# Last row-mode fetch moved ahead, mode sums joined before the root, a new order of tail loads and single-bank PSUM tiles in a two-layer block on a 512 x 512 x 64 image

## The chip, the cores and the metric

The kernel runs on one core of one Trainium2 chip. The metric is the device time of one execution in microseconds (us); before the change it is 1838.84 us, the median of three runs (1837.78 to 1840.75). The engines are named as in the profile: PE is the matrix engine (PEld its weight loads), DVE the vector engine, ACT the scalar engine, POOL the engine that here multiplies, adds and issues gathers, SP the engine that issues most of the DMAs.

## What is computed

The input x is 1 x 512 x 512 x 64 in fp32. Two layers follow one another, each added to its own input after a group norm with 32 groups of two channels over the whole image:

```python
x = x + conv0(gn(x), sequence_mask, ...)   # layer norm over channels, left and right projections with gates,
                                           # einsum('bkjd,bkid->bijd', left, right), layer norm, projection, output gate
x = x + conv1(gn(x), w_real, w_imag)

def conv1(x):                              # spectral convolution
    x_ft = fft2(x over rows, columns)[:12, :12]
    out_ft = einsum('bcmn,comn->bomn', x_ft, w_real + 1j * w_imag)
    return real(ifft2(out_ft put into zeros of 512 x 512))
```

Only 12 x 12 modes of the second layer's transform are kept, so it is done as matrix products with small tables of cosines and sines. Its group norm is linear in x except for its mean and scale: the modes are taken of the raw sums, and the scale (and at mode 0 the mean) is put in at the end. Both are known only once all of layer 0's output has been made. So the kernel ends with a stage in which nothing of the output can be written until the statistics and the modes of the whole image are there.

## The kernel before

The masked rows are fewer than 257 here, so the branch `compact` runs. Its main loop (about L1119 to L1231) walks over steps s, with k and n from `divmod(s, 8)`: n is the step within a unit of layer 0, and v counts the 32 output units, `last` being 31. A unit is one tile of 32 columns of the image by half of its rows. Inside this loop `tc.manual_schedule()` holds: each engine gets its instructions in the order in which the code writes them. In each step the code writes, among others, these pieces, each for its own unit and with its own delay:

- `times` (L979): the output gate's product w_ps on PE, for this step;
- `transform` (L1069): the row transform f_ps of the unit before, on PE at n = 0 and n = 4;
- the sigmoid on ACT (L1146) at even n; `gated` (L1038) and `added` (L1042) on POOL, and for the last quarter of the last unit `finished` (L1050, L1053) on DVE;
- `save` (L1077) copies f_ps on ACT and writes it to modes_d in DRAM (L1091), for the column tile before the last one on ACT's DMA queue; for the last column tile it goes straight on with 16 matmuls (L1083) into the PSUM tile `ends[0]`;
- `fetch(h)` (L904) reads a block of modes_d back with columns of the image on partitions, `columns(h)` (L896) transforms along the columns into t_ps; for h = 3 the block has 96 rows, comes on ACT's queue and is left open in `ends[0]`, so that L1083 adds the last 32 columns to it;
- `prepare` (L912): 24 small ACT operations, 6 in each of the steps n = 2 to 5 of the last unit, that spread the basis of the last column tile for L1083;
- `statistics` (L1097): DVE's batch statistics of the unit before; the joins L1102 to L1115 combine them;
- the gate's products z_t on DVE: `w_ps` by the factor (L1195) and the bias (L1201);
- `store` (L1058): layer 0's result to DRAM (x_h) by SP; `fetch_rows` (L629): a gather of a finished tile of x_h back into a buffer, issued by POOL, 15 of them ahead of their use (`AHEAD`). A buffer is one of four in the ring of `places`, in five tiles lx_t, in a spare piece, or earlier ones.
- w_real and w_imag, 2304 KB each, are read by SP (L1231) at v = last - 1, n = 3.

Behind the loop stands the tail (L1233 to L1372). It clears `picks` (L1237), lists the remaining load buffers and issues their gathers, loads three small tables, and calls `group_norm_affine` (L241) with the hook `turn_sums`. That sums the chunk means (`part`, L251), multiplies by an averaging matrix (mean_ps, L253), makes the mean (L255) and the variance (var_ps, L265), runs the hook (L1255 on DVE adds `ends[0]` to the sums, L1256 on PE turns them), then takes the inverse root (`rsqrt`) and picks each partition's own value. The rest joins the real and imaginary parts into v_modes (L1263, L1264), scales them into `picks` (L1267, L1273), multiplies by the mode weights (mixed_ps, L1282), sums (L1288, L1292), transforms back along the columns in `back_columns` (q_ps L1309, its copies L1320 on DVE and L1322 on ACT, transposes it_ps L1327, copies L1330 and L1332) and last, for 64 output tiles, along the rows (l_ps, L1348), adds to the loaded x (L1355) and stores (L1356); each tile issues the gather 15 tiles ahead.

Two lines of the call order matter for the change. In the loop:

```python
if (v, n) == (last, 4):
    fetch(3)
if (v, n) == (last, 7):
    ends.append(columns(3, ps_t))
```

These stand at the end of the code of a step, so behind that step's `times`, sigmoid, `prepare`, `statistics` and z_t products.

Of the kernel before, what the change touches and what calls it, by code (L numbers as in the profile page):

```python
# [46 lines left out]
def conv_preact_kernel(ctx: ExitStack, tc: tile.TileContext, t: dict):  # L47
# [192 lines left out]

    def group_norm_affine(keep, sets, each, name, between=lambda: None):  # L241


        groups, n = sets[0].shape[1:]
        avg = avg_p if groups == G else avg_c
        ab = keep.tile([P, 3], F32, name="ab_" + name)
        with tc.tile_pool(name="gn_" + name, bufs=1) as gp, tc.tile_pool(
            name="gnp_" + name, bufs=1, space=PSUM
        ) as gps:
            part = gp.tile([P, groups], F32, name="part")  # L250
            nc.vector.tensor_reduce(part, sets[0], AX.X, ALU.add)  # L251
            mean_ps = gps.tile([P, groups], F32, name="mean_ps")
            nc.tensor.matmul(mean_ps, avg, part, start=True, stop=True)  # L253
            mean = gp.tile([P, groups], F32, name="mean")
            nc.vector.tensor_scalar(mean, mean_ps, 1.0 / (n * each), None, ALU.mult)  # L255
            d = gp.tile([P, groups, n], F32, name="gn_d")
            nc.vector.scalar_tensor_tensor(
                d, sets[0], 1.0 / each, mean.unsqueeze(2).to_broadcast([P, groups, n]), ALU.mult, ALU.subtract
            )
            nc.vector.tensor_mul(d, d, d)  # L260
            nc.vector.scalar_tensor_tensor(d, sets[1], 1.0 / each, d, ALU.mult, ALU.add)
            v = gp.tile([P, groups], F32, name="v")
            nc.vector.tensor_reduce(v, d, AX.X, ALU.add)
            var_ps = gps.tile([P, groups], F32, name="var_ps")
            nc.tensor.matmul(var_ps, avg, v, start=True, stop=True)  # L265
            between()
            rs = rsqrt(gp, var_ps, 1.0 / n, EPS, [P, groups])
            if groups == G:
                mine = gp.tile([P, 2, G], F32, name="mine")
                nc.vector.tensor_mul(mine[:, 0, :], rs, pick)  # L270
                nc.vector.tensor_mul(mine[:, 1, :], mean, pick)
                am = gp.tile([P, 2], F32, name="am")
                nc.vector.tensor_reduce(am, mine, AX.X, ALU.add)
                rs, mean = am[:, 0:1], am[:, 1:2]
            nc.vector.scalar_tensor_tensor(ab[:, 1:2], mean, -1.0, rs, ALU.mult, ALU.mult)
            nc.vector.tensor_copy(ab[:, 0:1], rs)
            nc.vector.tensor_scalar(ab[:, 2:3], mean, -1.0, None, ALU.mult)
        return ab
# [334 lines left out]
    def compact(fc):  # L613
# [193 lines left out]
        with tc.tile_pool(name="tri", bufs=1) as trp:  # L807
# [57 lines left out]
            with tc.manual_schedule(), tc.tile_pool(name="late", bufs=1) as lp:  # L865
# [65 lines left out]
                with tc.tile_pool(name="np_x", bufs=LEAD + 2) as tp, tc.tile_pool(  # L931
# [189 lines left out]
                    for s in range(-LEAD, total_g + 2 * SIZE):  # L1121
# [101 lines left out]
                        if n == 6 and v % 8 == 3 and 8 < v < len(units):  # L1223
                            columns(v // 8 - 1, ps_t)
                        if (v, n) == (last, 4):
                            fetch(3)
                        if (v, n) == (last, 7):
                            ends.append(columns(3, ps_t))
# [4 lines left out]
                with tc.tile_pool(name="lq", bufs=1) as qp, tc.tile_pool(name="lx", bufs=1) as xp:  # L1233

                    picks = qp.tile([P, MODES, 3, 32], F32, name="picks")
                    fetch_rows(len(fetched))
                    nc.gpsimd.memset(picks, 0.0)  # L1237
                    buffers += [xp.tile([P, JC, C], F32, name=f"lx_t{i}") for i in range(5)]
                    buffers += [place(i)[:, r * JC : (r + 1) * JC] for i in (0, 1) for r in range(2)]
                    spare = places[:, 7 * 64 * C - 8 * 2 * MODES * M2 : 7 * 64 * C]  # L1240
# [9 lines left out]
                    with tc.tile_pool(name="sps", bufs=1, space=PSUM) as sps:  # L1250
# [9 lines left out]

                        ab2 = group_norm_affine(lp, sets, 8, "x1c", turn_sums)
                        v = qp.tile([P, 2, MODES, MODES], F32, name="v_modes")
                        nc.vector.tensor_add(v[:, 0], sums[:, :, :MODES], turned[:, :, MODES:])  # L1263
                        nc.vector.tensor_sub(v[:, 1], turned[:, :, :MODES], sums[:, :, MODES:])  # L1264
                        for k in range(2):
                            for q in range(3):
                                nc.vector.tensor_scalar(  # L1267
                                    picks[:, :, q, 12 * k + 4 * q : 12 * k + 4 * q + 4], v[:, k, :, 4 * q : 4 * q + 4],
                                    ab2[:, 0:1], None, ALU.mult,
                                )  # L1270
                            h = slice(k * C, (k + 1) * C)
                            one = picks[h, 0, 0, 12 * k : 12 * k + 1]
                            nc.vector.scalar_tensor_tensor(one, ab2[h, 1:2], float(N * N), one, ALU.mult, ALU.add)  # L1273

# [3 lines left out]
                        for m3 in range(3):  # L1278
                            for q in range(3):
                                for g in range(4):  # L1280
                                    m = MODES // 4 * g + m3
                                    nc.tensor.matmul(  # L1282
                                        mixed_ps[32 * g : 32 * g + 32, m3].rearrange("p (o g) r -> p o g r", g=4),
                                        picks[:, m, q, :], by_mode[:, :, :, m * MODES + 4 * q : m * MODES + 4 * q + 4],
                                        start=(q == 0), stop=(q == 2), tile_position=(0, 32 * g),
                                    )
                        own = picks.rearrange("p m q k -> p (m q k)")[:, : 3 * C * 4].rearrange("p (c r) -> p c r", r=4)
                        nc.vector.tensor_mul(  # L1288
# [11 lines left out]
                    def back_columns(jb, pq, pt, first):  # L1300

                        it = parts[:, jb // 2, : 256 * 16].rearrange("p (j o) -> p j o", o=16)
                        for g2 in range(2):
                            ps = pq.tile([P, 2, 4, 2, C], F32, name="q_ps")[:, :, :3]
                            for part in range(2):
                                for i in range(2):
                                    g = 2 * g2 + i
                                    h = slice(32 * g, 32 * g + M2)
                                    nc.tensor.matmul(  # L1309
                                        ps[:, i, :, part, :], col_inv[h, part, jb, :], mixed[h],  # L1310
                                        start=True, stop=True, tile_position=(32 * g, 0),
                                    )
                            for i in range(2):
                                g = 2 * g2 + i
                                src = ps[:, i].rearrange("p m k o -> p (m k) o")
                                for k, q in enumerate(qs):
                                    dst = q[:, :, 6 * g : 6 * g + 6].rearrange("p o r -> p r o")
                                    o = k * C // 2
                                    if first and k == 0:
                                        nc.vector.tensor_copy(dst, src[:, :, o : o + C // 2])  # L1320
                                    else:
                                        nc.scalar.copy(dst, src[:, :, o : o + C // 2])  # L1322
                        for o4 in range(4):
# [7 lines left out]
                            else:  # L1331
                                nc.scalar.copy(dst, ps)  # L1332
                    with tc.tile_pool(name="lpq0", bufs=2, space=PSUM) as pq, tc.tile_pool(
                        name="lpt0", bufs=4, space=PSUM
                    ) as pt:
                        back_columns(0, pq, pt, True)
                    with tc.tile_pool(name="lpq", bufs=1, space=PSUM) as pq, tc.tile_pool(
                        name="lpt", bufs=2, space=PSUM
# [103 lines left out]
```

## Time and profile before

| what | us |
|---|---|
| median of three runs | 1838.84 |
| profiled execution | 1839.54 |
| its span, first to last instruction | 1837.7 |
| PE busy | 1637.7 (89%) |
| DVE busy | 1423.6 (77%) |
| ACT busy | 961.9 (52%) |
| POOL busy | 945.3 (51%) |
| column transform L896 of the last fetch, start | 1501.48 |
| mean_ps L253, start | 1517.42 |
| mixed_ps L1282, start | 1526.97 |
| first copy of q_ps L1320, start | 1537.57 |
| first output store L1356, start | 1549.93 |

The profile is of one execution. The span is the time from its first instruction to its last. The rows of slices cut the span in 40 equal parts of 45.9 us; a digit is the share in tenths. The DMA row is the mean busy share of the 16 DMA engines. A timeline line has start, length, engine (with a q where it is the engine's DMA issue), line, operation, output and input with shapes, the count and in square brackets the idle time just before it with what ended it. A line of the chain has start, length and the piece. The clock row, PEclk, is the clock granted to PE as a share of full speed. Over the whole span DMA moves 467.94 MB in 188453 packets.

### The profile page before, as it was taken

The page shows a single profiled execution, that of the slowest core. Times are in us where ns is not written, and L with a number is a line of the kernel's source. Part 1 is how long each engine was busy: PE and PEld are TensorE (multiplying, and loading weights), DVE is VectorE, ACT ScalarE, POOL GpSimd, SP SyncE. Part 2 cuts the span into 40 slices and gives each one's busy share as a digit, 9 for nine tenths or more (in the row PEclk, how much of TensorE's full clock was granted, in tenths as well). Part 3 has the DMA queues.
Part 4 walks back from the last instruction along what each step waited for, and adds up shares of the span by engine and source line. Part 5 has one row for each costly group of instructions (what it writes and reads, how often), then busy time and mean ns, then how long its engine had stood idle before and what let it go on. Part 6 is the DMA issues. An engine that isn't in the chain of part 4 may idle for free.

```text
span 1837.7 us, 33577 instructions
## 1 busy us (share of the span) xinstructions
PE 1637.7 (89%) x11414; PEld 1287.7 (70%) x11414; DVE 1423.6 (77%) x2973; ACT 961.9 (52%) x1708; POOL 945.3 (51%) x711
## 2 busy tenths in 40 slices
PE   6779799999799999999999999999999866998772
PEld 5667666665678878897788888888888744665441
DVE  5989777777455547788999999999999975675552
ACT  3555555555222259976777777777777631111000
POOL 3666211111000006788999999999999862211110
PEclk9989899999899999999999999999999966555555
DMA  6999255556656513667777876776777698999999
GB/s 255 381 375 371 106 127 138 138 138 154 208 174 182 177 41 141 224 234 257 254 244 249 279 269 233 241 274 234 253 258 258 210 273 338 411 426 426 427 427 379
DMA packets 188453, 467.94 MB, mean 255 GB/s; under 512 B 34672, under 2 KB 134000, under 8 KB 147184
## 3 DMA queue, kind: packets, MB, share of 16 engines
q1 hardware_dynamic: 157376, 262.21, 42.5%
q0 software_dynamic: 27712, 201.40, 29.1%
q10 hardware_dynamic: 3184, 2.08, 0.4%
q8 instruction: 93, 1.52, 0.3%
q14 instruction: 88, 0.72, 0.1%
HBM read 278.05 MB, written 187.56 MB: 253 GB/s over the span
## 4 chain that ended last, share of the span: by engine, by line
PE 29%; DVE 16%; DMA 9%; POOL 4%; issue 3%; ACT 1%; DVEq 0%; POOLq 0%; ACTq 0%
PE c_ps L979 6%; PE w_ps L979 6%; PE t_ps L969 5%; PE l_ps L1348 4%; DVE stats2c L1097 4%; DMA places<-x_h,dst_i 4%; PE y_ps L990 4%; DVE z_t L1195 3%; DVE scratch L1012 3%; DVE z_t L1201 3%; PE f_ps L1069 2%; POOL z_t L1038 2%; DMA out_x<-places 2%; POOL places L1042 2%; DMA lx_t<-x_h,dst_i 2%
## 5 line engine op out<-in xcount | busy, mean ns | idle before, releaser
L979 PE MATMUL w_ps<-gate_x,xt_c 128*128 128x128 f32 x2048 | 280.1, 280 | 32.1 <-DVE z_t L1195 26.7
L1042 POOL TENSOR_TENSOR places<-places,z_t 128x1024 f32<-128x1024 f32 x127 | 301.2, 2371 | 8.0
L979 PEld LDWEIGHTS w_ps<-gate_x,xt_c 128*128 128x128 f32 x2048 | 251.5, 194 | 47.8 <-DVE z_t L1195 43.4
L979 PE MATMUL c_ps<-center_x,xt_c 128*128 128x128 f32 x2048 | 276.2, 278 | 1.2 <-ACT xt_c L1008 0.6
L979 PEld LDWEIGHTS c_ps<-center_x,xt_c 128*128 128x128 f32 x2048 | 252.1, 194 | 3.9 <-ACT xt_c L974 2.3
L1348 PE MATMUL l_ps<-places,rinv 24*128 24x512 f32 x512 | 207.8, 1124 | 29.3 <-DVE places L1355 18.6
L1097 DVE BATCH_NORM_STATS2 stats2c<-places 128x6 f32<-128x128 f32 x1024 | 220.5, 278 | 12.5 <-POOL places L1042 12.5
L1012 DVE TENSOR_REDUCE scratch<-sq_c 128x16 f32<-128x1024 f32 x160 | 194.6, 1216 | 27.9 <-ACT sq_c L1007 18.7
L1146 ACT ACTIVATE z_t<-z_t 128x1024 f32<-128x1024 f32 x128 | 135.5, 1059 | 133.7 <-DVE z_t L1201 116.0
L1199 POOL TENSOR_TENSOR z_t<-z_t,bias_row_out 128x1024 f32<-128x1024 f32 x32 | 75.7, 2365 | 246.6 <-DVE z_t L1195 242.5
L969 PE MATMUL t_ps<-c_ident,places 128*128 128x128 f32 x1280 | 199.0, 278 | 1.3 <-DVE places L854 1.3
L1348 PEld LDWEIGHTS l_ps<-places,rinv 24*128 24x128 f32 x512 | 120.3, 303 | 111.9 <-DVE places L1355 59.6
L969 PEld LDWEIGHTS t_ps<-c_ident,places 128*128 128x128 f32 x1280 | 144.5, 142 | 60.6 <-issue 50.3
L974 ACT ACTIVATE xt_c<-t_ps,ab_xc 128x512 f32<-128x512 f32 x256 | 176.0, 687 | 10.7 <-PE t_ps L969 9.8
L1195 DVE TENSOR_TENSOR z_t<-w_ps,rs_n 128x512 f32<-128x512 f32 x256 | 171.9, 672 | 3.7 <-PE w_ps L979 3.5
L1004 ACT ACTIVATE sq_c<-c_ps 128x512 f32<-128x512 f32 x256 | 150.5, 588 | 30.9 <-PE c_ps L979 29.4
L679 DVE BATCH_NORM_STATS2 stats1c<-x_ps 128x6 f32<-128x512 f32 x256 | 155.6, 681 | 12.5 <-PE x_ps L678 12.2
L1201 DVE TENSOR_TENSOR z_t<-z_t,scratch 128x1024 f32<-128x1024 f32 x128 | 156.3, 1221 | 10.0 <-ACT rs_n L1018 3.8
L1038 POOL TENSOR_TENSOR z_t<-z_t,places 128x1024 f32<-128x1024 f32 x64 | 151.6, 2369 | 16.2 <-ACT z_t L1146 13.3
L1355 DVE TENSOR_TENSOR places<-places,l_ps 128x512 f32<-128x512 f32 x176 | 110.2, 683 | 56.1 <-DMA places<-x_h,dst_i 45.5
L1038 POOL TENSOR_TENSOR z_t<-z_t,bias_row_out 128x1024 f32<-128x1024 f32 x63 | 149.4, 2371 | 4.6 <-ACT z_t L1146 4.0
L733 POOL COPY rbc<-rq_out 128x512 f32<-128x512 f32 x64 | 38.3, 613 | 210.0 <-DVE rq_out L209 132.0
(212 smaller groups left out, 2748.8 us busy)
## 6 DMA issues: line engine op xcount, KB each, us to landing
x_h<-places SPq DMA_DIRECT2D x64, 1024.0 KB
out_x<-places SPq DMA_DIRECT2D x44, 1024.0 KB
places<-u_d SPq DMA_DIRECT2D x512, 64.0 KB
out_x<-lx_t SPq DMA_DIRECT2D x20, 1024.0 KB
left_d<-o_c SPq DMA_DIRECT2D x64, 256.0 KB
right_d<-o_c SPq DMA_DIRECT2D x64, 256.0 KB
left_raw<-left_d SPq DMA_DIRECT2D x64, 256.0 KB
right_raw<-right_d SPq DMA_DIRECT2D x64, 256.0 KB
```

The source lines that it names most:

```text
L679: nc.vector.bn_stats(stats[:, 0, 16 * (jc % quarter) + 4 * r + c, :], ps.rearrange("p i k -> p (i k)"))
L969: nc.tensor.transpose(tps[:, i, :], flat[:, o : o + P], ident)
L974: nc.scalar.activation(xts[s], tps, AF.Identity, bias=ab1[:, 2:3])
L979: nc.tensor.matmul(ps[:, 2 * i : 2 * i + 2, :], xts[s][:, i, :], w, start=True, stop=True)
L1004: nc.scalar.activation(sq, cps, AF.Square)
L1012: nc.vector.tensor_reduce(totals[k % 2][:, 8 * (n - 1) : 8 * (n + 1)], sqs.pop(s // 2), AX.X, ALU.add)
L1038: nc.gpsimd.tensor_mul(zs[k, c], zs[k, c], u)
L1042: nc.gpsimd.tensor_add(xr, xr, zs.pop((k, c)))
L1097: nc.vector.bn_stats(st[k // 4][:, g, k % 4, :], x_of(k)[:, :, 2 * g : 2 * g + 2])
L1195: nc.vector.tensor_mul(z[:, 8 * odd : 8 * odd + 8, :], wps, rs)
L1201: nc.vector.tensor_add(z, z, bias_ps["ogate"].unsqueeze(1).to_broadcast([P, 16, C]))
L1348: nc.tensor.matmul(ps.rearrange("p j o -> p (j o)"), rinv[h, b, :], it[h], start=True, stop=True, tile_position=(32 * g, 0),)
```

## The change

1. In the last unit, `fetch(3)` stands in the code of n = 0 instead of n = 4, and `columns(3)` in that of n = 6 instead of n = 7.
2. `group_norm_affine` has two hooks. `with_mean` runs after the mean's product, and gets `turn_sums`. `with_variance` runs after the variance's product and before the root; the partition's own mean is picked before it, and it gets the new `join_modes`: the two v_modes operations and the two that put the mean in at mode 0 (into v, ahead of the scale). After the root, only the scale is picked and multiplied in. `picks` has a row of 108 places for a mode (three blocks of 36, with a window of 32 at 32 q), so that two operations of 128 x 144 take the place of six of 128 x 48 and two one-element ones.
3. The list of load buffers begins with the two halves of place 0, then the five lx_t, then place 1 and the spare piece; before, the five lx_t came first.
4. Each q_ps group has its own PSUM tile of one bank (four buffers for the first `back_columns`, two later); before, two groups shared a tile of two banks. In the first `back_columns`, DVE copies both halves of one group and ACT both of the other; before, DVE copied one half of each and ACT the other.

```diff
-    def group_norm_affine(keep, sets, each, name, between=lambda: None):
+    def group_norm_affine(keep, sets, each, name, with_mean=lambda: None, with_variance=lambda ab: None):
...
             nc.tensor.matmul(mean_ps, avg, part, start=True, stop=True)
+            with_mean()
...
             nc.tensor.matmul(var_ps, avg, v, start=True, stop=True)
-            between()
+            if groups == G:
+                mine = gp.tile([P, 2, G], F32, name="mine")
+                nc.vector.scalar_tensor_tensor(mine[:, 1, :], mean, -1.0, pick, ALU.mult, ALU.mult)
+                nc.vector.tensor_reduce(ab[:, 2:3], mine[:, 1, :], AX.X, ALU.add)
+            else:
+                nc.vector.tensor_scalar(ab[:, 2:3], mean, -1.0, None, ALU.mult)
+            with_variance(ab)
             rs = rsqrt(gp, var_ps, 1.0 / n, EPS, [P, groups])
             if groups == G:
-                mine = gp.tile([P, 2, G], F32, name="mine")
                 nc.vector.tensor_mul(mine[:, 0, :], rs, pick)
-                nc.vector.tensor_mul(mine[:, 1, :], mean, pick)
-                am = gp.tile([P, 2], F32, name="am")
-                nc.vector.tensor_reduce(am, mine, AX.X, ALU.add)
-                rs, mean = am[:, 0:1], am[:, 1:2]
-            nc.vector.scalar_tensor_tensor(ab[:, 1:2], mean, -1.0, rs, ALU.mult, ALU.mult)
-            nc.vector.tensor_copy(ab[:, 0:1], rs)
-            nc.vector.tensor_scalar(ab[:, 2:3], mean, -1.0, None, ALU.mult)
+                nc.vector.tensor_reduce(ab[:, 0:1], mine[:, 0, :], AX.X, ALU.add)
+            else:
+                nc.vector.tensor_copy(ab[:, 0:1], rs)
+            nc.vector.tensor_mul(ab[:, 1:2], ab[:, 2:3], ab[:, 0:1])
...
-                        if (v, n) == (last, 4):
+                        if (v, n) == (last, 0):
                             fetch(3)
-                        if (v, n) == (last, 7):
+                        if (v, n) == (last, 6):
                             ends.append(columns(3, ps_t))
...
-                    picks = qp.tile([P, MODES, 3, 32], F32, name="picks")
+                    picks = qp.tile([P, MODES, 3 * 36], F32, name="picks")
...
-                    buffers += [xp.tile([P, JC, C], F32, name=f"lx_t{i}") for i in range(5)]
-                    buffers += [place(i)[:, r * JC : (r + 1) * JC] for i in (0, 1) for r in range(2)]
+                    for i in (0, 1):
+                        buffers += [place(i)[:, r * JC : (r + 1) * JC] for r in range(2)]
+                        if i == 0:
+                            buffers += [xp.tile([P, JC, C], F32, name=f"lx_t{j}") for j in range(5)]
...
-                        ab2 = group_norm_affine(lp, sets, 8, "x1c", turn_sums)
                         v = qp.tile([P, 2, MODES, MODES], F32, name="v_modes")
-                        nc.vector.tensor_add(v[:, 0], sums[:, :, :MODES], turned[:, :, MODES:])
-                        nc.vector.tensor_sub(v[:, 1], turned[:, :, :MODES], sums[:, :, MODES:])
+
+                        def join_modes(ab):
+                            nc.vector.tensor_add(v[:, 0], sums[:, :, :MODES], turned[:, :, MODES:])
+                            nc.vector.tensor_sub(v[:, 1], turned[:, :, :MODES], sums[:, :, MODES:])
+                            for k in range(2):
+                                h = slice(k * C, (k + 1) * C)
+                                one = v[h, k, 0, 0:1]
+                                nc.vector.scalar_tensor_tensor(one, ab[h, 2:3], float(N * N), one, ALU.mult, ALU.add)
+
+                        ab2 = group_norm_affine(lp, sets, 8, "x1c", turn_sums, join_modes)
                         for k in range(2):
-                            for q in range(3):
-                                nc.vector.tensor_scalar(
-                                    picks[:, :, q, 12 * k + 4 * q : 12 * k + 4 * q + 4], v[:, k, :, 4 * q : 4 * q + 4],
-                                    ab2[:, 0:1], None, ALU.mult,
-                                )
-                            h = slice(k * C, (k + 1) * C)
-                            one = picks[h, 0, 0, 12 * k : 12 * k + 1]
-                            nc.vector.scalar_tensor_tensor(one, ab2[h, 1:2], float(N * N), one, ALU.mult, ALU.add)
+                            nc.vector.tensor_scalar(
+                                picks.rearrange("p m (q f) -> p m q f", q=3)[:, :, :, 12 * k : 12 * k + 4],
+                                v[:, k].rearrange("p m (q j) -> p m q j", q=3), ab2[:, 0:1], None, ALU.mult,
+                            )
...
-                                        picks[:, m, q, :], by_mode[:, :, :, m * MODES + 4 * q : m * MODES + 4 * q + 4],
+                                        picks[:, m, 32 * q : 32 * q + 32], by_mode[:, :, :, m * MODES + 4 * q : m * MODES + 4 * q + 4],
...
-                            ps = pq.tile([P, 2, 4, 2, C], F32, name="q_ps")[:, :, :3]
+                            pair = [pq.tile([P, 4, 2, C], F32, name="q_ps")[:, :3] for _ in range(2)]
...
-                                        ps[:, i, :, part, :], col_inv[h, part, jb, :], mixed[h],
+                                        pair[i][:, :, part, :], col_inv[h, part, jb, :], mixed[h],
...
-                                src = ps[:, i].rearrange("p m k o -> p (m k) o")
+                                src = pair[i].rearrange("p m k o -> p (m k) o")
...
-                                    if first and k == 0:
+                                    if first and i == 0:
                                         nc.vector.tensor_copy(dst, src[:, :, o : o + C // 2])
...
-                    with tc.tile_pool(name="lpq0", bufs=2, space=PSUM) as pq, tc.tile_pool(
+                    with tc.tile_pool(name="lpq0", bufs=4, space=PSUM) as pq, tc.tile_pool(
...
-                    with tc.tile_pool(name="lpq", bufs=1, space=PSUM) as pq, tc.tile_pool(
+                    with tc.tile_pool(name="lpq", bufs=2, space=PSUM) as pq, tc.tile_pool(
```

## The prediction

> **What bounds the kernel now.** I read first the page's slices, then a table of stretches of the tail, then the chain of waits in order of time, then the timeline of the last two units. In the slices, the row of DMA shares:
>
> ```profile
> DMA  6999255556656513667777876776777698999999
> ```
>
> The DMA is full in the last eight slices but for one dip. The stretches (length, busy time of PE, PEld, DVE, ACT, POOL, then clock, DMA share, GB/s) show where it is not:
>
> ```profile
> 1490.00:1495.00 5.00, 0.00 (x0) 0.00 (x0) 4.57 (x13) 2.36 (x4) 4.92 (x3) 0.50 0.80 159
> 1540.00:1545.00 5.00, 3.65 (x16) 3.27 (x16) 2.47 (x3) 2.26 (x3) 0.00 (x0) 0.50 0.83 346
> 1545.00:1550.00 5.00, 3.92 (x14) 2.05 (x15) 2.48 (x4) 0.26 (x1) 0.00 (x0) 0.50 0.04 16
> 1550.00:1837.70 287.70, 220.73 (x598) 134.13 (x594) 157.39 (x252) 20.02 (x36) 45.89 (x49) 0.51 0.99 413
> ```
>
> From the first output store (1549.93) to the end the DMA is full: 64 stores and 49 loads of 1 MB each. Just before, it is empty: all early loads have landed and no store has begun. So the end is the first store plus a constant 288 us, and what counts is when the first store comes. The chain leads back from it:
>
> ```profile
> 1485.32 16.11 DMA places<-modes_d
> 1501.48 5.31 PE t_ps L896 x24
> 1506.80 3.67 PE f_ps L1069 x16
> 1510.49 0.59 ACT places L1077
> 1511.12 6.37 PE t_ps L1083 x32
> 1517.49 0.60 PE mean_ps L253 x2
> ```
>
> The mean waits on PE behind L1083 and everything ahead of it, and that waits for the last fetch of row modes. The statistics path is ready earlier: `part`, L251, is done at 1512.82, while mean_ps runs at 1517.42. It is next in line, 4.6 us behind. The timeline says how the fetch came to take 16 us, and what else stands near:
>
> ```profile
> 1468.40 1.80 ACTq L1091 DMA_DIRECT2D modes_d<-places  x4
> 1478.80 1.06 ACT L1146 ACTIVATE z_t<-z_t 128x1024 f32<-128x1024 f32 x1 [2.94 <-DVE z_t L1201]
> 1481.52 0.47 SPq L1231 DMA_DIRECT2D places<-in_w_imag  x1
> 1485.32 0.33 ACTq L904 DMA_DIRECT2D places<-modes_d  x1
> 1487.91 1.68 PE L979 MATMUL w_ps<-gate_x,xt_c 128*128 128x128 f32 x8 [0.21 <-DVE z_t L1195]
> 1491.18 0.68 DVE L1195 TENSOR_TENSOR z_t<-w_ps,rs_n 128x512 f32<-128x512 f32 x1
> 1501.48 5.31 PE L896 MATMUL t_ps<-col_basis,places 96*128 96x24 f32 x24 [11.89 <-DMA places<-modes_d]
> 1526.71 0.16 DVE L1273 SCALAR_TENSOR_TENSOR picks<-ab_x1c,picks 64x1 f32<-64x1 f32 x1 [1.77 <-DVE picks L1267]
> 1537.57 0.48 DVE L1320 COPY q_sb<-q_ps 128x192 f32<-128x192 f32 x1 [1.68 <-PE q_ps L1309]
> 1538.09 0.48 ACT L1322 COPY q_sb<-q_ps 128x192 f32<-128x192 f32 x1 [26.47 <-DVE q_sb L1320]
> ```
>
> The modes_d writes that the fetch reads are issued at 1468.40 to 1470.2, but w_imag and the last unit's stores, which wait for the first and the last of them, leave SP at 1481.52 and 1482.73: the writes lie behind w_real (2304 KB, 64 packets, issued 1461.95), and their queue moves its packets between 1476.4 and 1481.4. So fetch(3), wherever it stands, cannot issue before 1481.5 to 1482.7. Before, ACT issued it at 1485.32.
>
> **What the Trainium skill says.** "DMA: Bandwidth & Descriptors", section "Queues, rings and completion order": each DMA engine goes round its queues packet by packet and drains a whole packet before it turns. The trace agrees: w_imag's four packets per engine end at about 1483.1, 1485.5, 1488.3 and 1491.3 to 1494, and of the fetch's 112 packets 5 move in 1490 to 1494, 58 in 1494 to 1498, 49 until 1501.4. "TensorE: Matmul & The Clock Gate", part 2: matmuls stay in program order, only weight loads are pulled ahead; its part 1: after an idle window the array runs at half clock. The trace shows 0.50 after 1490. "PSUM — Partial Sum Buffer", section "PSUM bank collisions raise a hardware error": reads of one bank by two engines are kept apart by a dependency. The trace shows L1320 and L1322 strictly in turn.
>
> **Part 1: fetch and columns moved.** The fetch issues at 1482.0 to 1482.7 instead of 1485.32, 3 us earlier. ACT reaches it at 1475.9, right behind the last unit's first sigmoid, and waits; the next sigmoid (1478.80) slips to about 1482.5, and the 12 spreads behind it (4.26 us), then POOL's products: POOL is busy throughout, so it slips 0.6 to 1.2 us, off the path. The fetch arrives during w_imag's first packets instead of its third. As the later fetch did, it lets about two pass first, sends one packet per engine near 1491, a second before 1494; the remaining 80 or so go at the 14.5 per us that 58 in 4 us gave, against the same stores and gather: 5.5 to 6.3 us, so landing L = 1499.5 to 1500.3. I take L = 1500.3. Bounds: 1494.5 if w_imag alternates fairly from its first packet, 1501.4 if the start gains nothing.
>
> The columns now stand on PE between w_ps of the last unit's n = 6 and n = 7; before, after both. So w_ps(n=7), done by 1489.6 in the cover of the fetch, now waits for the fetch too, and behind it DVE's z_t (1491.18), the sigmoid, L1050, L1053 and 40 statistics (end 1504.49: 13.3 us from z_t on). Step by step: columns L to L+5.35 (5.31 measured); w_ps at half clock 1.97 (1.68 measured at mixed clock), z_t at L+7.3; 13.3 to the end of the statistics, L+20.6; joins 1.6 (1504.49 to 1506.10); square .6 on ACT, which before stood queued behind the save; between .5, part .4 and its gaps, L+24.1; mean L+24.8. L1083 ends only at about L+20.6 (w_ps, f_ps 3.7, save .6, L1083 6.4 and gaps), so statistics decide. Before, mean was at 1518.12. With L = 1500.3 it is 1525.1: 7.0 later. The clear loss of part 1.
>
> **Part 2: sums and mean joined ahead of the root.** Mean to `v` stays 2.02 us (1518.12 to 1520.14): L+26.8. The picked mean, its sum, v_modes (.21 each step) and two one-element operations run while var_ps is made, and push the root .6: it starts at L+27.9, lasts 1.98 (1520.64 to 1522.62), L+29.9. After it stand one product, a sum, a product and two picks of 128x144: 1.27 from the like rows, mixed_ps at L+31.15. Before: root end to mixed_ps 4.35 us, of which 1.77 is the stall in front of L1273 beside a POOL gather. So 2.3 to 2.5 net, 0.7 if such a stall comes back. Price bounds: -2.5 to -0.5.
>
> **Part 3: PSUM tiles.** Copies of q_ps go from 3.4 us in turn (1537.57 to 1540.95) to two engines side by side, 1.5 us: the first it_ps starts 1.75 earlier, bounds 0 (PE or clock takes it) to 1.9.
>
> **Part 4: load order.** Place 0's loads need only the statistics of unit 30 and its store; lx_t need `part` as before. Two megabyte loads move from after lx_t to about L+14. Hidden: the nine loads finish at about 1549, still before the first store; 3 us margin. Uncovered it would be 4.9 us per load and store pair. The larger memset (+0.13 us by 1296 to 1152 elements) lies in POOL's idle 13 us. Cost 0.
>
> **Sum.** mixed_ps before 1526.97, after L+31.15 = 1531.45: +4.5. Part 3: -1.75. First store 1549.93 + 2.7 = 1552.6; span 1837.7 + 2.7 = 1840.4, execution 1839.54 + 2.7 = 1842.2. That execution is .7 above the median of 1838.84; on the median 1841.5. In one line: change = L - 1497.6.
>
> **Rivals.** 0.2% is 3.7 us, about what measurement can tell from no change.
> (a) My forecast: L 1498.5 to 1501.2, +1 to +3.7: 1841.5. Chance .40. For it: the packet pattern; against: two queues' phase is one sample.
> (b) Other side, slower: the fetch gains nothing, or the stall before the picks comes back, or the PSUM gain is lost. L = 1501.4 gives +3.8, 1842.7; with a stall of 1.77 on top 1844.4. It decides from L = 1501.3. For it: x_h stores and two gathers meet the fetch at the same time as before (DMA 348 GB/s in 1495 to 1500). Chance .35.
> (c) Faster: the fetch gets its turns ahead of w_imag and lands by 1488, when w_ps(n=7) is due at 1487.91. Then the change is 1488 - 1497.6 = -9.6: 1829. It decides below L = 1493.9. Against: ACT cannot issue before 1481.5, and w_imag is out by then. Chance .14.
> (d) L 1494 to 1498.5: 1837, no difference. Chance .08.
> (e) The change doesn't reach the end, because the stores are DMA bound whatever the first one does: 1838.8. Against it the hole of 16 GB/s. Chance .03.
>
> **How the numbers follow.** Faster .14 (c), same .51 (a, d, e), slower .35 (b). Range 1834 to 1846.5: it leaves out most of (c), some .12, and .06 above, where stalls add up. The likeliest case's own range is 1839.8 to 1842.5.
>
> **What the changed profile would show.** Right: ACT issues the fetch at 1482 to 1483 right before a late sigmoid; PE's columns wait for places<-modes_d with w_ps behind them; DVE idles before the last z_t to about 1507; L1083 no longer ends last before mean_ps, the statistics do; statistics end near 1521; no gap before the picks; L1320 and L1322 overlap; the hole of the DMA before the first store, now near 1552.6. Wrong: a fetch that lands before 1494, or w_ps(n=7) ahead of the columns (then the change is at least 7 us better), or a hole filled by late loads.

## The result and the profile after

The changed kernel takes 1842.53 us, the median of 15 runs (1841.11 to 1845.06), and the kernel before 1834.81 us over 15 runs (1832.5 to 1841.76): ratio 1.0035, 95% interval 1.0024 to 1.0045, which is 6.4 us slower (0.0035 x 1834.81; 4.4 to 8.3). The time forecast was 1841.5, and the range 1834 to 1846.5; the forecast change was only +2.7 us, under the 3.7 us that the forecast took for what can be told from no change. So the time came out nearly as stated while the change came out more than twice as large. Both can be, since the median of before that the forecast started from (1838.84, three runs) is 4.0 us above the median of fifteen. That the time lies only 1.0 us from the forecast is therefore luck: a start 4.0 us too high and a change 3.7 us too small nearly cancel.

In the profile after (execution 1844.57 us, span 1842.8) the whole program has moved against the first profile of before by 3.7 us before the change's first instruction: w_real is issued at 1465.67 instead of 1461.95. Over the profiles of this study that issue lies anywhere between 1458.75 and 1466.46, whatever the kernel. So times within the tail are given below from the issue of w_real.

The timeline of the changed kernel, with the lines that answer to those shown of before (line numbers are those of its own file, up to 9 larger):

```profile
1465.67 0.52 SPq L1234 DMA_DIRECT2D places<-in_w_real  x1
1485.17 0.47 SPq L1234 DMA_DIRECT2D places<-in_w_imag  x1
1485.73 0.38 ACTq L907 DMA_DIRECT2D places<-modes_d  x1
1486.21 1.06 ACT L1149 ACTIVATE z_t<-z_t 128x1024 f32<-128x1024 f32 x1 [6.64 <-POOL places L1045]
1504.69 5.31 PE L899 MATMUL t_ps<-col_basis,places 96*128 96x24 f32 x24 [13.29 <-DMA places<-modes_d]
1509.83 2.06 PE L982 MATMUL w_ps<-gate_x,xt_c 128*128 128x128 f32 x8
1511.92 0.69 DVE L1198 TENSOR_TENSOR z_t<-w_ps,rs_n 128x512 f32<-128x512 f32 x1 [16.95 <-PE w_ps L982]
1517.45 7.81 DVE L1100 BATCH_NORM_STATS2 stats2c<-places 128x6 f32<-128x128 f32 x40
1528.86 0.61 PE L253 MATMUL mean_ps<-part,c_avg_p 128*128 128x32 f32 x2 [5.39 <-DVE part L251]
1546.19 1.45 DVE L1329 COPY q_sb<-q_ps 128x192 f32<-128x192 f32 x4 [1.02 <-PE q_ps L1318]
1546.23 1.45 ACT L1331 COPY q_sb<-q_ps 128x192 f32<-128x192 f32 x4 [18.70 <-PE q_ps L1318]
1555.51 8.88 SPq L1365 DMA_DIRECT2D out_x<-places  x4
```

The order that the forecast gave is there. ACT issues the fetch right behind w_imag, and its sigmoid has waited 6.64 us. PE stands 13.29 us for the fetch, with w_ps behind the columns; DVE stands 16.95 us for that w_ps. The statistics end at 1525.26, and mean_ps now waits for DVE's `part`, no more for the 32 products of L1083 (here L1086), which end at 1523.48. The two engines copy q_ps at the same time.

The chain of waits of the changed kernel leads from the statistics to `part` and the mean, where before it had columns, transform, save and L1083 ahead of the mean. Its last steps:

```profile
1528.30 0.43 DVE part L251
1528.73 0.14 issue
1528.86 0.62 PE mean_ps L253 x2
```

One sign went the other way. The forecast expected the DMA hole ahead of the first store to stay, with the loads of x done 3 us before it, and named a hole filled by late loads as a sign of being wrong. In before's first profile DMA was 0.04 busy there; here it is busy almost to the store:

```profile
1550.00:1555.00 5.00, 3.14 (x18) 1.87 (x17) 3.01 (x5) 1.46 (x2) 0.00 (x0) 0.84 0.93 385
```

The loads that wait for `part` are issued 12 us later after w_real than in before, and the last of them end about 0.5 us ahead of the store. It cost nothing that can be seen: from the first store to the end it is 287.3 us; in before, 287.8. The hole is no fixed part of the kernel before either (see e1).

### The profile page after: what moved, and what is told of

It reads as the page before. It is cut to its first block, busy times and chain, and to the rows that moved or that the text cites. A ratio compares the mean times of both kernels' runs of the same rounds, so it can differ in the third digit from the quotient of the medians.

```text
span 1842.8 us, 33577 instructions
## 1 busy us (share of the span) xinstructions
PE 1639.4 (89%) x11414; PEld 1289.6 (70%) x11414; DVE 1423.9 (77%) x2968; ACT 961.3 (52%) x1708; POOL 945.2 (51%) x711
```

## The experiments

Parts are numbered as in the prediction: part 3 is the PSUM tiles (item 4 in "The change"), part 4 the load order (item 3). Each kernel was timed in turn with before on the same chip, but not all on one chip, so that a difference between two of them is a difference of two ratios to before; changes in us are the ratio's difference from 1 times the median of before there (1832.8 to 1836.4).

### e1: before, once more (no edit)

> The kernel before, unchanged, for a second profile of it and for what two equal programs differ by. Theory T (the tail's order of work explains the change): ratio 1.000 within 0.001; the tail from the issue of w_real to the first output store is 88.0 us long (1461.95 to 1549.93 in the first profile), within 1 us. Rival R (the first profile of before was an unlucky one, and most executions of before have a shorter tail): the same tail is 3 us or more shorter, the fetch of 96 row modes landing nearer to 10 us after its issue than 16.

Measured: ratio 0.9996 (0.9986 to 1.0007). The second profile of the very same program has a tail 6.2 us shorter: 1460.81 to 1542.61, 81.8 us, against 88.0. Of its chain of waits:

```profile
1484.21 16.04 DMA places<-modes_d
1500.29 5.32 PE t_ps L896 x24
1505.61 3.20 PE f_ps L1069 x16
1508.83 0.59 ACT places L1077
1509.47 4.17 PE t_ps L1083 x32
```

T held for the ratio and fell for the tail. The fetch takes as long as in the first (16.04 and 16.11), so rival R was right that the tail can be shorter, and wrong on the cause. The difference up to the mean, 3.0 us, shows first in the transform (3.20 instead of 3.67 us), and for the most part at L1083: 4.17 instead of 6.37 us. The stretches that span L1083, of before's first profile and of this second one, give the clock (the column after POOL's busy time):

```profile
1511.12:1517.42 6.30, 6.30 (x32) 3.95 (x33) 1.13 (x3) 0.50 (x2) 3.38 (x4) 0.64 0.76 228
```

```profile
1509.47:1513.57 4.10, 4.10 (x33) 3.25 (x33) 1.14 (x3) 0.49 (x2) 1.79 (x2) 1.00 1.10 344
```

The granted clock was 0.64 there and 1.00 here, for the same 32 products. The 0.64 is a mean of 0.50 and a late 1.00 in before's first profile; in the second profile the clock was still 0.50 in the transform, and rose ahead of L1083:

```profile
1511.12:1515.60 4.48, 4.48 (x20) 2.90 (x22) 1.13 (x3) 0.50 (x2) 1.88 (x2) 0.50 0.70 209
1515.70:1517.42 1.72, 1.72 (x16) 0.94 (x13) 0.00 (x0) 0.00 (x0) 1.42 (x2) 1.00 0.93 276
```

```profile
1505.70:1508.05 2.35, 2.35 (x12) 0.43 (x12) 0.00 (x0) 0.00 (x0) 0.00 (x0) 0.50 1.00 422
```

So it rose 14.2 us after the columns' start in the one and 7.8 in the other. In each of the fourteen profiles all changes of the granted clock lie whole multiples of 3.41 us apart, and where this grid falls differs from one execution to the next. Seven profiles keep before's order on PE and have the columns at 5.3 us. In four of them (e1, e3, e6, e7) a grid point fell 7.7 to 8.3 us after the columns' start, the clock rose there, and L1083 took 4.17 us. In three (before's first, e4, e8) the grid points fell at 6.3 to 7.4 and again at 9.7 to 10.8, the clock rose only at 13.1 to 14.2, and L1083 took 5.8 to 6.4 us. So the first profile of before was no rare accident, but one of two kinds that come about equally often here. That the place of the grid decides is read from these seven; no run here moves it.

The points of the tail, in us after w_real's issue:

| | before, first profile | before, second | changed |
|---|---|---|---|
| columns of the fetch start | 39.5 | 39.5 | 39.0 |
| mean | 56.2 | 53.2 | 63.8 |
| mixing (mixed_ps) | 65.0 | 60.3 | 70.0 |
| q_ps | 74.1 | 68.5 | 79.6 |
| it_ps | 78.6 | 72.4 | 81.8 |
| l_ps | 83.4 | 77.2 | 86.2 |
| first store | 88.0 | 81.8 | 89.8 |

Between mean and mixing another 1.7 us go: the stall of 1.77 us in front of L1273 isn't there in the second profile. Of six profiles with the old order of these operations (before twice, e2, e7, e8, e10) two have it (before's first and e8), and their mean to mixing is 8.9 and 8.8 us; the others have 7.1 to 7.5.

In the second profile the DMA is nearly without a hole, with no later loads: the loads run nearly up to a first store that simply comes earlier (1542.61, 81.8 us after w_real):

```profile
1537.00:1542.60 5.60, 3.85 (x13) 2.01 (x14) 2.57 (x5) 0.94 (x1) 0.00 (x0) 0.50 0.84 348
```

The changed kernel's first store is 8.0 us after that of the second profile, and 1.9 us after that of the first. The measured 6.4 lies between the two, nearer the second.

### e2: part 1 alone

```diff
-                        if (v, n) == (last, 4):
+                        if (v, n) == (last, 0):
                             fetch(3)
-                        if (v, n) == (last, 7):
+                        if (v, n) == (last, 6):
                             ends.append(columns(3, ps_t))
```

> Before with part 1 alone: fetch(3) at n = 0 and columns(3) at n = 6 of the last unit; joins, load order and PSUM tiles as before. T: the mean comes 7 us later and nothing gives it back: +7.0 us, ratio 1.0038 (+5.5 to +8). If the rest of the change only looks like a gain in the tail and is worth nothing at the end (rival N), e2 equals the changed kernel: +6.4, ratio 1.0035, and e3 equals before.

Measured: 1.0047 (1.0032 to 1.0062), +8.6 us. The mean comes 63.8 us after w_real, exactly where it comes in the changed kernel; against before's second profile that is 10.6 us later, against the first 7.6. T's +7.0 was the cost against the first profile; the measured 8.6 lies between the two. Rival N said +6.4 here and 0 for the next kernel; this one's interval (+5.9 to +11.4) doesn't exclude it, the next one's does.

### e3: the change without part 1

> The changed kernel with part 1 undone: fetch(3) at n = 4 and columns(3) at n = 7 as before; the joined sums, the load order and the PSUM tiles stay. T: mean_ps waits for L1083 as in before, then 2.3 us less to the mixing and 1.8 us less in the copies: -3.5 to -4.1 us, ratio 0.998. Rival N: 0, ratio 1.000. Rival M (something outside of the tail makes the changed program start its main loop later, as its profile shows a shift of 3.7 us before the change's first instruction): 0 to +2 us with the shift of 3.7 us in its profile again.

Its edit is the diff above, backwards, on the changed kernel. Measured: 0.9976 (0.9965 to 0.9986), -4.4 us. T is right, N and M are out: the other three parts make the kernel faster, and part 1 more than takes it away (10.8 us between the two ratios, 6.4 + 4.4). In its profile the fetch lands 38.8 us after w_real, the mean comes at 52.8, and the shift of the main loop is not there (w_real at 1461.05). The chain from the mean on is shorter by what the steps said and by one thing more, in the timeline:

```profile
1530.96 1.94 PE L1336 MATMUL it_ps<-c_ident,q_sb 128*128 128x128 f32 x16 [1.24 <-ACT q_sb L1331]
1534.00 1.14 PE L1357 MATMUL l_ps<-places,rinv 24*128 24x512 f32 x8 [1.10 <-ACT places L1341]
```

In before's profiles these two took 3.65 and 2.09 us. PE is granted its full clock here (1.00 in 1530 to 1535).

### e4: only the columns put back behind w_ps

```diff
-                        if (v, n) == (last, 6):
+                        if (v, n) == (last, 7):
                             ends.append(columns(3, ps_t))
```

on the changed kernel; the fetch stays early.

> The changed kernel with columns(3) alone put back to n = 7, behind the last product w_ps; the fetch stays at n = 0. T: no wait on the statistics' path any more; the fetch lands 0.5 us earlier than in before, so -4 to -4.7 us against before, 10 us better than the changed kernel: ratio 0.9977. If the early fetch itself costs (the sigmoid behind it on ACT is late, and POOL with it, rival A): between -1 and +3.

Measured: 0.9965 (0.9953 to 0.9977), -6.4 us against before (-8.6 to -4.2; T had said -4 to -4.7). Against the changed kernel that is 12.8 us from the place of one call. Of these the two profiles show 9.6: the first store comes 80.3 us after w_real instead of 89.8, and the mean 54.8 instead of 63.8, although L1083, back on the path, had a clock of 0.70 in this profile and took 5.8 us. Its timeline shows w_ps of both last steps ahead of the wait, and the columns alone behind it:

```profile
1478.89 0.38 ACTq L907 DMA_DIRECT2D places<-modes_d  x1
1483.37 3.68 PE L982 MATMUL w_ps<-gate_x,xt_c 128*128 128x128 f32 x16 [1.47 <-DVE z_t L1198]
1497.67 5.32 PE L899 MATMUL t_ps<-col_basis,places 96*128 96x24 f32 x24 [10.63 <-DMA places<-modes_d]
```

The early fetch lands 38.9 us after w_real, later fetches 38.8 (e3) and 39.5 (before, twice): from issue to landing it takes 18.8 us instead of 15.4 to 16.1. Issuing it 3 us earlier gains next to nothing, and rival A (-1 to +3) is out: the intervals of this kernel and of e3 overlap and show no cost of the early fetch.

### e9: w_imag behind the fetch, in the changed kernel

```diff
-                        if v == last - 1 and n == 3:
-                            for part, name in enumerate(("w_real", "w_imag")):
-                                nc.sync.dma_start(wide[part * C : (part + 1) * C], ...)
+                        if v == last - 1 and n == 3:
+                            mode_weights(0, "w_real")
...
                         if n == 6 and v - 1 == last:
-                            for r in range(2):
-                                store(last, r)
+                            store(last, 0)
+                            mode_weights(1, "w_imag")
+                            store(last, 1)
```

> The changed kernel with only the load of w_imag moved, from right behind w_real to between the last unit's two stores, so that it can't be issued before the fetch of the row modes. T (w_imag's packets hold the fetch back, and the fetch holds w_ps): the fetch lands 5 to 7 us after its issue instead of 19, the columns no longer make w_ps late by more than 4 us, and the changed order costs next to nothing: -4 to -8 us against before, 11 to 16 us better than the changed kernel. Rival S (the stores and gathers hold the fetch, w_imag doesn't matter): as the changed kernel, +6 to +8.

Measured: 0.9977 (0.9969 to 0.9985), -4.2 us against before. From its timeline:

```profile
1482.36 0.33 ACTq L907 DMA_DIRECT2D places<-modes_d  x1
1489.16 5.06 PE L899 MATMUL t_ps<-col_basis,places 96*128 96x24 f32 x24 [0.92 <-DMA places<-modes_d]
1494.05 2.05 PE L982 MATMUL w_ps<-gate_x,xt_c 128*128 128x128 f32 x8
1494.96 0.48 SPq L1059 DMA_DIRECT2D places<-in_w_imag  x1
```

The fetch lands 6.8 us after its issue instead of 19.0, with the first of the last unit's stores and the gathers about as before: w_imag held it. The changed order of PE is still in place, but PE waits 0.92 us for the fetch, and the change becomes a gain, at the low end of T's range. Rival S is out.

### e10 and e14: PE kept busy until the fetch lands

```diff
+                    for _ in range(24 if h == 3 else 0):
+                        nc.tensor.matmul(
+                            ps.rearrange("p m n -> p (m n)"), turn, sums.rearrange("p m n -> p (m n)"), start=True, stop=True
+                        )
                     for m in range(MODES):
                         nc.tensor.matmul(ps[:, m, :], by[:q, m, :], col_basis[:q, h, :], ...)
```

once on before and once on the changed kernel.

> Before with 24 extra products of turn and sums (128 x 288 each, overwritten by what follows) on PE ahead of columns(3), in the time in which PE waits for the fetch; nothing else. T2 (the clock of PE at the landing of the fetch sets how long columns, transform and L1083 take, and is why before's first profile was 6 us longer in the tail than its second): mean_ps no later than 13 us after the columns' start, -1 to -3 us against before, and no spread of several us between executions of the tail. Rival C (the clock is no matter, or the products don't hold it): 0, or later if they outlast the wait.

Measured on before: 0.9981 (0.9969 to 0.9992), -3.5 us. The columns take 2.86 instead of 5.3 us, and mean_ps starts 12.5 us after them (first and second profile of before: 15.9 and 13.3). But the clock, 1.00 through the columns, fell to 0.50 within the transform behind them; L1083 ran at 0.66 in this profile and took 6.2 us, and the first store (81.6 us after w_real) is no earlier than in before's second profile. So the gain and the shorter columns of T2 are shown; that the spread of the tail would go is not: L1083 can still meet the low clock, and the times lie between 1825.9 and 1835.9 us.

> The changed kernel with the 24 extra products ahead of columns(3), as in e10, so that PE stays at full clock until the fetch lands. T: columns 2.9 instead of 5.3 us and w_ps 1.2 instead of 2.1, both on the path of the changed kernel: 3.3 us better than it, so +3 to +5 against before, ratio 1.0020. Rival: the clock of PE is no part of the loss, +6.4 as the changed kernel.

Measured on the changed kernel: 1.0023 (1.0014 to 1.0032), +4.2 us (2.6 to 5.9), so some 2.2 of its 6.4 us (4.4 to 8.3) gone, though the intervals overlap. In the profiles the first store comes 2.1 us earlier (87.8 instead of 89.8 us after w_real). Its columns and w_ps, from the timeline:

```profile
1503.34 2.76 PE L903 MATMUL t_ps<-col_basis,places 96*128 96x24 f32 x24
1505.93 1.68 PE L986 MATMUL w_ps<-gate_x,xt_c 128*128 128x128 f32 x8
```

The statistics end 56.5 us after w_real, in the changed kernel 59.6: 3.1 of the 3.3 us that were expected at that point.

### e7, e6 and e8: each of the other parts alone, on before

> Before with part 3 alone, each q_ps group in a PSUM bank of its own. T as predicted: the copies end 1.75 us sooner: -1.8 us, ratio 0.9990. T2, after the profile of the kernel without part 1 (where the transposes it_ps also took 1.94 instead of 3.65 us): the shorter gap also leaves PE at full clock in what follows, -3 to -4.4 us, ratio 0.998. Rival N: 0.

Part 3 (the q_ps hunks of the diff): 0.9980 (0.9971 to 0.9988), -3.7 us. The copies are over sooner by what was forecast (q_ps to it_ps 2.19 us instead of 3.96 in before's second profile). The time is in T2's range, but its own profile shows the faster clock only in part, with it_ps at 3.15 us and l_ps at 2.09: 1.76 and 0.5 us together are 2.3, just inside the interval (-5.3 to -2.2). In the six profiles without part 3, it_ps took 3.65 us each time; in the eight with it, 1.9 to 3.7, and 1.94 only in e3.

> Before with part 2 alone (sums and mean joined ahead of the root, two wide picks). As predicted: -2.5 us, ratio 0.9986. After the second profile of before, in which no stall of 1.77 us stands ahead of the picks and mean to mixing is 7.1 us instead of 8.9: -0.9 us, ratio 0.9995, mean to mixing 6.2 us. Rival N: 0.

Part 2 (the hunks of `group_norm_affine`, `join_modes` and `picks`): 0.9996 (0.9984 to 1.0007), no difference that can be told. Mean to mixing is 6.28 us, and 6.2 to 6.3 in all eight profiles with the new order, so 0.9 us less than the undisturbed 7.1, and the stall was in none of them.

> Before with part 4 alone (place 0's loads ahead of lx_t). As predicted: 0, ratio 1.000 within 0.001; the two gathers issue right after the memset of picks (near 37 us after the issue of w_real) instead of after the lx_t. Rival G (the two early megabytes lie in the way of the fetch or of the tables): +1 to +3. Rival H (they fill the hole of the DMA before the first store): -1 to -3.

Part 4 (the hunk of `buffers`): 0.9985 (0.9975 to 0.9995), -2.8 us, where the forecast said 0. Rival G is out, and the size is that of rival H, but the profile doesn't bear out H's reason: in the 6.7 us before the first store DMA was 0.00 busy, so the hole was there, and longer than in before's first profile. The two gathers issue 41.6 and 45.9 us after w_real instead of behind the lx_t, but the mean comes at 54.9, the stall ahead of the picks is back (1.50 us), and the first store comes at 86.7 us, with 287.7 from there to the end. This profile is of the slowest of its executions (1841.24 us, the others down to 1832.29), so it says little about the median. The measured gain is small and stays unexplained.

### e12 and e13: towards a faster kernel

> Joined sums, load order and PSUM tiles of the change; fetch(3) at n = 4 and columns(3) at n = 7 as before; w_imag between the last unit's two stores. T: the fetch lands about 5 us after its issue, PE has done columns and L1083 before the statistics end, and the mean comes 5 us earlier than in the kernel without part 1, where PE's chain set it: -8 us against before (-6 to -10), ratio 0.9956. Rival D (DMA is full anyhow, and what is loaded later only shifts): as the kernel without part 1, -4.4. Rival S: -4.4 as well, with the fetch landing 16 us after its issue.

This is e3 with w_imag moved as in e9. Measured: 0.9965 (0.9953 to 0.9977), -6.4 us. The fetch lands 5.5 us after its issue, and the mean comes 46.6 us after w_real, 6.2 earlier than in e3. Of this only 2.9 reach the first store (73.7 against 76.6), as a new wait stands behind:

```profile
1524.25 1.55 PE L1321 MATMUL q_ps<-mixed,col_inv 24*128 24x192 f32 x16 [3.92 <-DMA col_inv<-in_c_col_inv]
```

and from the first store to the end it is 290.9 us instead of 286.0, with DMA full up to the first store and 2.3 MB more to move after it (121.8 instead of 119.5). So rival D is right for the greater part; the measured 2.0 us between e12 and e3 are within the intervals.

The next kernel put the three small tables on SP's queue and cleared q_sb ahead of the loads:

```diff
-                    nc.scalar.dma_start(col_inv, t["c_col_inv"])
+                    nc.sync.dma_start(col_inv, t["c_col_inv"])      # pick4 and rinv likewise, ahead of the loads
```

> The kernel with w_imag late and n = 4, n = 7 (e12), with the three small tables on SP's queue ahead of the loads instead of on ACT's behind the joins, and the clearing of q_sb ahead of the loads on POOL. T: q_ps no longer waits 3.9 us for col_inv: first store 2 us sooner, -8 us against before, ratio 0.9955. Rival D (from there on DMA carries the end): as e12, -6.4.

Measured: 0.9963 (0.9951 to 0.9975), -6.8 us, not to be told from e12. T fell: col_inv still came late (q_ps waited 4.23 us for it). On SP's queue it was issued 37 us after w_real, 8 us earlier than in e12, but behind w_imag and the last store; that these held it is likely and not shown. e4, e12 and e13 all beat both kernels, by about the same.

## Why the prediction was right, and where its size was off

- **What bounds the kernel, and that the end follows the first store.** Right: from first store to end it is 287.8 us in both profiles of before and 287.3 after. It holds less well where loads are still running at the first store (290.9 in e2 and e12, 290.1 in e9).
- **The fetch cannot issue before 1481.5 to 1482.7, and w_imag holds it.** Right. It was issued 20.1 us after w_real, which is 1482.0 on before's clock, and the columns started at 39.0, which is 1501.0 instead of the 1500.3 taken: the earlier fetch gained 0.5 us instead of 1.2. e9 shows that w_imag is the cause.
- **w_ps(n=7) and the statistics wait behind the columns.** Right, and it is the whole loss (e4). The steps after the landing L were forecast as L + 7.3, 20.6, 24.8 and 31.15 for z_t, the end of the statistics, the mean and the mixing; they measured 7.2, 20.6, 24.8 and 31.0. Then 19.8 us to the first store, where the forecast had 21.2: q_ps to l_ps and the store were at a higher clock, while the mixing took longer (7.5 us with a gap, 6.1 in before's second profile; not explained).
- **"Before, mean was at 1518.12 ... 7.0 later. The clear loss of part 1."** This is the term that was mis-sized. 1518.12 was that of an execution in which L1083 took 6.37 us at a clock of 0.64. In the second profile it took 4.17, and the mean came 3.0 us earlier after w_real; part 1 cost 10.6 us there. Measured it cost 8.6 us alone (e2) and 10.8 beside the other parts, instead of 7.0. The old path of the mean led through PE, whose clock was at 0.50 after the wait and rose sooner or later, and varied with it; in the changed kernel L1083 ends ahead of `part`, so that a good clock at L1083 gains nothing.
- **The other three parts together** were forecast at -4.2 us (-2.5 and -1.75) and measured -4.4 (e3), so that the miss of the sum, 3.7, is that of part 1. Taken singly they were off, and in ways that cancel; the three single measurements add up to -7.2, more than e3, with intervals of about 2 us each way.
- **"So 2.3 to 2.5 net, 0.7 if such a stall comes back."** The stall stood in two of six profiles of the old order, and the forecast took it for the rule. The gain of the order itself is 0.9, and alone it can't be told from none.
- **PSUM tiles, 1.75 us.** 1.76 in e7's profile against before's second; the measured 3.7 (2.2 to 5.3) is more. That PE gets its full clock sooner behind the shorter gap adds 0.5 us in that profile (it_ps) and may add more in others (e3); it isn't shown for the rest.
- **Load order, 0.** Measured -2.8 (-0.9 to -4.6); open. That the loads would be done 3 us ahead of the first store was wrong: in the changed kernel it was about 0.5 us, which cost nothing.
- **The rivals.** (a) was the mechanism that happened, with L in its range; by its own formula L = 1501.0 gives +3.4. But its time was taken against one execution of the slower kind, so that the change ended in the size of (b), of whose causes only the poor gain of the fetch was there, for 0.7 us. (c) is what e9 brings about by moving the transfer. (e) is out for a change of this size: the first store moved and the end with it. That there is such a limit is seen in e12, where most of what the mean gained did not reach the end.

What stays open: why the load order alone gains, what sets the place of the 3.41 us grid of PE's clock in an execution, what the stall ahead of L1273 waits for, and 3.2 of the 12.8 us between the changed kernel and e4, which their two profiles don't show.

## What to carry to other kernels

A call that waits for a transfer must stand, on an in-order engine, behind all that another path needs: here one line's place was worth 12.8 us (9.6 in the profiles), and moving the transfer's issue without asking what it queues behind was worth next to nothing. When the quantity to be predicted is a few us, one profile isn't a baseline; take a second one, ask of each stage on the path whether its duration depends on the clock or on an occasional stall, and state a step's loss against both kinds of execution.

## What was not expected of the hardware

The same 32 products took 6.37 us in one execution and 4.17 in the next, at granted clocks of 0.64 and 1.00, after waits for the fetch of about the same length (11.89 and 12.33 us). The granted clock changed only on a grid of 3.41 us, and rose 7.8 us after the columns' start in one execution and 14.2 us after it in the other, though PE was busy in nearly all of that time. A fetch of 0.59 MB behind a transfer of 2304 KB in 64 packets took 19.0 us from its issue to the start of what waited for it, and 6.8 us without it. Extra work on PE during such a wait nearly halved what came right after it (5.3 to 2.8 or 2.9 us for the columns), at no cost to the kernel's time.
